# Routing by sequence inside the chunked streams, and expert results normed by sequence beside the shared expert and the last attention

## The chip, the cores and the metric

The kernel runs on one NeuronCore of a Trainium2 chip. The metric is the device time of the whole program in microseconds (us). All times below are in us unless they say otherwise, and times on the profile's clock count from the start of the profiled span.

The engines have short names in the profile: PE multiplies matrices (PEld loads its weights), DVE works on vectors, ACT evaluates activation functions, POOL is the general engine that also issues the indirect transfers, and SP issues most of the other transfers. Each engine takes its instructions in a fixed order and waits for semaphores of the others.

## The reference, cut to what matters

The network has eight layers, each of the form x = layernorm(x + f(x)), in fp32, on 8 sequences of 256 tokens with 128 channels (2048 tokens in all). The sixth layer's f is a chunked attention block, the seventh is a mixture of experts, and then come an attention with 16 heads and a linear layer with ternary weights. The seventh and what surrounds it are what the change touches:

```python
def _L2_ffn_ref(x, router_w, rg, ru, rd, sg, su, sd):
    ...                                   # E, K = 8, 2; capacity = 320 for T = 2048 tokens
    xn = xf * jax.lax.rsqrt(jnp.mean(xf * xf, axis=-1, keepdims=True) + eps)
    logits = xn @ router_w.T
    probs = jax.nn.softmax(logits, axis=-1)
    topk_p, topk_i = jax.lax.top_k(probs, K)
    rw = topk_p / jnp.sum(topk_p, axis=-1, keepdims=True)
    ...
    order = jnp.argsort(~sel, axis=1, stable=True)
    dispatch = order[:, :capacity]        # the first 320 tokens that chose the expert
    ...
    xg = xf[dispatch]
    gate = jax.nn.silu(jnp.einsum('ech,ehi->eci', xg, rg))
    up = jnp.einsum('ech,ehi->eci', xg, ru)
    eout = jnp.einsum('eci,eih->ech', gate * up, rd)
    ...
    routed = jnp.zeros_like(xf).at[dispatch.reshape(-1)].add(contrib.reshape(-1, h))
    shared = jax.nn.silu(x @ sg) * (x @ su) @ sd
    return shared + SCALE * routed.reshape(b, s, h)
...
x = _layernorm(x + _L2_ffn_ref(...), axis=-1)
x = _layernorm(x + _L3_attn_ref(...), axis=-1)
x = _layernorm(x + _L3_ffn_ref(...), axis=-1)
```

A token's place in its expert's list is the number of earlier tokens that chose the same expert. Each token is used by two of eight routed experts (128 to 512 to 128 channels), as long as the place is within the capacity of 320, and by the shared expert (128 to 1024 to 128).

## The kernel before

Activations lie by channel: 128 partitions of channels, 2048 columns of tokens. A tile is 128 tokens, so there are 16 tiles and two per sequence. Six stages run one after the other: `rglru`, `local_mamba`, `moe1`, `chunked`, `moe2`, `typed`. The builder writes a program; a scheduler then sets the order of the instructions on each engine by cost estimates of its own, within the data dependences. `issue_after(later, earlier)` adds an order constraint and `wait_for` a real wait. `psum(tag)` hands out the eight banks of the accumulation memory, split by tags that each stage sets in `BANKS`.

**chunked.** `one_sequence(b)` is one sequence's generator: attention, feed-forward, attention, feed-forward, each followed by a norm. The planner `on_pe` keeps three of them in flight: each `yield` names the PE time of the next piece and how long its result lies behind, and the planner runs the piece that is ready first. The norm by token (`normed`) gives `z`, tokens by channels. `put_rows` writes `z` to a DRAM tensor `rows2` in token order on SP's queue; the sum of squares goes into `ssq` (ACT), and `logits` multiplies the normed activations with the router on PE ("lg") and copies the result into `lg2` (DVE, line 817).

**moe2.** It begins when the last logits are there. On DVE, for all 16 tiles at once, `first_best` takes the best and the second expert, `places` counts places with matmuls "cum" and "tot" and a scan, `slots` turns them into row numbers of the experts' lists, and `dispatch` inverts the map: it compares each place with 128 numbers (line 1115, eight operations of 512 columns) and lets 32 matmuls "which" sum up the token that belongs in each of the 2560 slots. `rows_of` then reads the rows of the tokens from `rows2` by 20 indirect gathers of 128 rows on POOL (line 1147), twelve at first and four after each group, and `group` transposes four of them to channels. Quarters 0 and 1 of the shared expert are issued before the experts. A quarter is `shared(i)`: 512 tokens in 8 chunks, each with the matmuls "pg" and "pu", a silu on ACT and a multiply on DVE (lines 1534 and 1535), and the matmul "acc". The eight experts follow, with their outputs written to `ybuf2` on SP's queue. Then 32 gathers (two per tile) fetch each token's two results. Quarters 2 and 3 of the shared expert run, and `combine` scales and adds the two results of four tiles (lines 1581 and 1582), transposes them (line 1584) and adds them to a quarter's sum; `issue_after` holds these operations behind chunk 4 of the fourth quarter, or a quarter's last. Four layernorms of 512 columns close the stage.

**typed.** Each sequence has six units of scores. In step i of the loop the transposes of unit i-3, the scores of unit i, the softmax of unit i-1 and the outputs of unit i-3 are issued. Between them run side generators, one `next` at two places in the step: `before(b)` (`typed_inputs`: projections "proj", the rotation on DVE with its addition on POOL, the masked keys "km" on POOL, line 1667, and the values) and `after(b, o)` (output projection, layernorm, linear layer, layernorm, output). When the last unit of sequence b is done, `after(b, o)` is appended and `before(b + 2)` behind it. Softmax multiplies its exponentials by 1/sum on POOL (line 1715).

**moe1**, which already routes in parts (`route1`): the rows of each tile are scattered on POOL (line 1058) directly into the experts' places in DRAM, and the places are then read with plain transfers ("got<-places") into the groups.

## Time and profile before

| | us |
|---|---|
| median of 3 runs | 1897.03 (1895.95 to 1901.52) |
| the profiled execution | 1904.73, span 1903.0 |
| mean granted PE clock | 0.91 |
| PE / DVE / ACT / POOL busy in the span | 1571.1 / 1073.6 / 1009.9 / 549.8 |
| last logits of chunked | 1405.6 to 1406.6 |
| routing on DVE | 1406.6 to 1425.8 |
| first expert's first matmul, last expert's last | 1469.4, 1537.0 |
| result gathers | 1540.5 to 1580.2 |
| first scores of typed | 1632.5 |
| scores' start, one sequence to the next, in typed | 33.5 |

The busy time of an engine is the sum of its instructions' durations; PE's instructions overlap, so PE being busy does not mean that it runs at its peak. "Idle before" is the time in which an engine stood ahead of an instruction, with what released it. The granted clock says at what share of the full speed PE's clock ran; a matmul at half clock takes about twice as long.

### The profile page before, as it was taken

The page shows a single profiled execution, that of the slowest core. Times are in us where ns is not written, and L with a number is a line of the kernel's source. Part 1 is how long each engine was busy: PE and PEld are TensorE (multiplying, and loading weights), DVE is VectorE, ACT ScalarE, POOL GpSimd, SP SyncE. Part 2 cuts the span into 40 slices and gives each one's busy share as a digit, 9 for nine tenths or more (in the row PEclk, how much of TensorE's full clock was granted, in tenths as well). Part 3 has the DMA queues.
Part 4 walks back from the last instruction along what each step waited for, and adds up shares of the span by engine and source line. Part 5 has one row for each costly group of instructions (what it writes and reads, how often), then busy time and mean ns, then how long its engine had stood idle before and what let it go on. Part 6 is the DMA issues. An engine that isn't in the chain of part 4 may idle for free. (4 is left out here: it accounts for less than half of the span.)

```text
span 1903.0 us, 28168 instructions
## 1 busy us (share of the span) xinstructions
PE 1571.1 (83%) x10805; PEld 944.4 (50%) x10805; DVE 1073.6 (56%) x1830; ACT 1009.9 (53%) x2657; POOL 549.8 (29%) x483
## 2 busy tenths in 40 slices
PE   3678877887888776786679999999969986898987
PEld 2344544444454433443556666776634642455554
DVE  5734567786878677589224444463452223565654
ACT  4557777676877867454234444554422311454544
POOL 1324452515161414203221010000003042445552
PEclk6689999989999988788789999999979997998998
DMA  3000012121111112266300000000011310000000
GB/s 146 1 1 1 1 35 56 35 56 35 56 41 49 50 41 71 93 198 180 103 24 2 7 7 4 4 4 4 4 37 24 108 39 13 1 4 6 4 7 6
DMA packets 56822, 74.11 MB, mean 39 GB/s; under 512 B 5493, under 2 KB 34360, under 8 KB 55664
## 3 DMA queue, kind: packets, MB, share of 16 engines
q1 hardware_dynamic: 52800, 66.60, 12.0%
q0 software_dynamic: 2832, 5.19, 1.1%
q8 instruction: 85, 1.39, 0.3%
q10 hardware_dynamic: 1056, 0.52, 0.1%
q14 instruction: 49, 0.40, 0.1%
HBM read 65.55 MB, written 7.35 MB: 38 GB/s over the span
## 5 line engine op out<-in xcount | busy, mean ns | idle before, releaser
L396 PE MATMUL y<-hs,ident 128*128 128x512 f32 x256 | 148.4, 710 | 38.3 <-DVE hs L791 38.3
L790 DVE TENSOR_TENSOR_SCAN hs<-da,hs 128x1024 f32<-128x1024 f32 x64 | 148.7, 2332 | 3.5 <-ACT da L786 3.0
L477 PE MATMUL pt<-ident,e 128*128 128x128 f32 x768 | 120.9, 285 | 28.3 <-POOL e L653 17.3
L786 ACT ACTIVATE da<-d,na 128x255 f32<-128x255 f32 x256 | 112.1, 502 | 36.8 <-DVE hs L790 19.3
L653 POOL TENSOR_TENSOR e<-e,rc 128x1024 f32<-128x1024 f32 x32 | 72.2, 2255 | 201.4 <-DVE rc L652 201.3
L1335 POOL TENSOR_TENSOR e<-e,rc 128x512 f32<-128x512 f32 x32 | 33.6, 1052 | 331.9 <-DVE rc L1334 225.6
L1712 ACT ACTIVATE e<-sc,nm 128x128 f32<-128x128 f32 (+1 forms) x256 | 104.2, 435 | 47.7 <-DVE nm L1707 47.2
L648 ACT ACTIVATE e<-sc,nm,rn 128x128 f32<-128x128 f32 x256 | 113.5, 464 | 24.1 <-DVE nm L643 23.9
L1715 POOL TENSOR_TENSOR e<-e,rc 128x1024 f32<-128x1024 f32 x48 | 91.9, 1916 | 111.6 <-DVE rc L1714 73.9
L477 PEld LDWEIGHTS pt<-ident,e 128*128 128x128 f32 x768 | 87.6, 143 | 73.4 <-POOL e L653 24.8
L479 ACT COPY ptsb<-pt 128x512 f32<-128x512 f32 x82 | 48.1, 587 | 141.0 <-PE pt L477 72.5
L600 POOL TENSOR_TENSOR t<-t,t 128x512 f32<-128x512 f32 x64 | 89.1, 1393 | 96.7 <-DVE t L587 88.1
L788 DVE TENSOR_TENSOR hs<-u,bc 128x1024 f32<-128x1024 f32 x64 | 86.5, 1360 | 41.3 <-POOL u L775 26.2
L396 PEld LDWEIGHTS y<-hs,ident 128*128 128x128 f32 x256 | 52.4, 220 | 94.9 <-DVE hs L791 51.7
L1310 ACT COPY kp<-kps 128x512 f32<-128x512 f32 x128 | 74.7, 586 | 41.0 <-PE kps L396 40.8
L479 DVE COPY ptsb<-pt 128x512 f32<-128x512 f32 x110 | 73.7, 683 | 36.6 <-PE pt L477 30.9
L1707 DVE TENSOR_REDUCE nm<-sc 128x4 f32<-128x1024 f32 (+1 forms) x48 | 58.6, 1221 | 51.3 <-PE sc L396 51.2
L396 PE MATMUL qk<-w_local,h 128*128 128x512 f32 x128 | 72.6, 655 | 17.8 <-DVE t L587 13.0
L791 DVE TENSOR_TENSOR hs<-hs,bc 128x1024 f32<-128x1024 f32 x64 | 81.9, 1287 | 0.2
L1534 ACT ACTIVATE sh<-pg 128x512 f32<-128x512 f32 x32 | 19.1, 597 | 102.8 <-PE pg L396 69.2
L1346 DVE COPY vs<-vps 128x512 f32<-128x512 f32 x64 | 42.3, 671 | 52.5 <-PE out L396 31.1
L396 PE MATMUL sc<-km,q 64*128 64x512 f32 x192 | 62.8, 722 | 8.8 <-POOL km L1667 8.7
(425 smaller groups left out, 3797.4 us busy)
## 6 DMA issues: line engine op xcount, KB each, us to landing
bc<-xs SPq DMA_DIRECT2D x128, 256.0 KB
w_attn<-in_w_dram SPq DMA_DIRECT2D x4, 1024.0 KB
w_local<-in_w_dram SPq DMA_DIRECT2D x2, 1557.0 KB
w_moe<-in_e1gate_dram SPq DMA_DIRECT2D x8, 256.0 KB
w_moe<-in_e1up_dram SPq DMA_DIRECT2D x8, 256.0 KB
w_moe<-in_e1down_dram SPq DMA_DIRECT2D x8, 256.0 KB
w_moe<-in_e2rg_dram SPq DMA_DIRECT2D x8, 256.0 KB
w_moe<-in_e2ru_dram SPq DMA_DIRECT2D x8, 256.0 KB
```

The source lines that it names most:

```text
L396: return self.nc.tensor.matmul(out, lhsT, rhs, start=start, stop=stop)
L477: self.last = self.nc.tensor.transpose(pt[:, j * P : (j + 1) * P], src[:, j * P : (j + 1) * P], self.ident)
L479: self.nc.any.tensor_copy(sb.rearrange("p a b -> p (a b)"), pt)
L600: nc.gpsimd.tensor_add(t1, t1, t2)
L648: nc.scalar.activation(e[:, j, g, :], scs[:, j, g, :], AF.Exp, bias=nm[:, j, g : g + 1], scale=rq[:, j, g : g + 1], accum_out=sm[:, j, g : ...
L786: nc.scalar.activation(da[:, n, c, 1:S], d[:, c, 1:S], AF.Exp, scale=na[:, i : i + 1])
L788: nc.vector.tensor_tensor(hs, u.unsqueeze(1).to_broadcast(shp), bn, ALU.mult)
L790: nc.vector.tensor_tensor_scan(line(hs), line(da), line(hs), 0.0, ALU.mult, ALU.add)
L791: nc.vector.tensor_tensor(hs, hs, cn, ALU.mult)
L1310: nc.scalar.copy(k[:, 2 * i : 2 * i + 2, :].rearrange("p a b -> p (a b)"), ps)
L1712: nc.scalar.activation(e[:, i, :], sc[:, i, :], AF.Exp, bias=nm[:, i : i + 1], accum_out=sm[:, i : i + 1])
L1715: nc.gpsimd.tensor_tensor(e, e, rc.unsqueeze(2).to_broadcast([P, n, keys]), ALU.mult)
```

## The change

Four things change.

1. *Routing.* `route2(b, z, work, small)` is called at the end of each sequence in chunked. It scales the logits of two tiles, takes best and second expert, computes places from a running sum over the earlier sequences (`sum2`) with three small matmuls "cum", and scatters the two tiles' rows of `z` twice (four indirect transfers on POOL) into `places[1]` in DRAM. The combined `scatter` serves moe1 as well. `put_rows`, `first_best`, `places`, `slots`, `dispatch` and the gathers of rows go away, and so do their tables. `places[1]` is cleared at the start of the program, as `places[0]` was, by a second transfer of 1280 KB.
2. *Reading the rows.* `rows_of(pool, k)` serves both mixtures: five plain transfers, alternating between SP's and ACT's queue, that wait for all the scatters.
3. *The shared expert.* Its weights are loaded in chunked, into the space of the first attention's folded weights, once the last sequence is past them (`weights_shared`). Quarter 0 is ahead of the experts, quarters 1 to 3 behind.
4. *Results and typed.* `results(b, work)` combines, transposes and norms one sequence (256 columns). Sequence 0's results, the inputs of typed for sequence 0 and sequence 1's results are taken a step at a time between the chunks of quarters 2 and 3; results of b+2 are side generators in typed, appended with the first output unit of sequence b. At the last unit of sequence b the first step of `after` is taken, and `before(b + 2)` is appended ahead of its rest. There are three side steps per unit in place of two. The order of the combining operations is no longer held by `issue_after`. The pools of typed are opened at the start of moe2, so that the memsets of `vm` are in moe2. moe2 has its own split of banks.

```diff
+    def route2(self, b, z, work, small):
+        ...
+        nc.scalar.activation(rs, self.ssq[:, ts], AF.Ln, scale=1.0 / P, bias=float(np.finfo(np.float32).eps))
+        nc.scalar.activation(rs, rs, AF.Exp, scale=-0.5)
+        ...
+        nc.vector.tensor_tensor(lg, lg, each(rs), ALU.mult)
+        for k in range(2):
+            o = oh[:, k]
+            nc.vector.tensor_reduce(mx[:, k], lg, AX.X, ALU.max)
+            nc.vector.tensor_tensor(o, lg, each(mx[:, k]), ALU.is_equal)
+            nc.vector.tensor_tensor(o, o, io, ALU.mult)
+            nc.vector.tensor_reduce(ix[:, k], o, AX.X, ALU.min)
+            nc.vector.tensor_tensor(o, io, each(ix[:, k]), ALU.is_equal)
+            if k == 0:
+                nc.vector.scalar_tensor_tensor(lg, o, NEG, lg, ALU.mult, ALU.add)
+        sel = small.tile([P, 2, E], BF, tag="sel", name="sel", bufs=2)
+        nc.vector.tensor_tensor(sel, oh[:, 0], oh[:, 1], ALU.add)
+        cum = self.psum("M", "cum")[:, 0 : 2 * E].rearrange("p (t e) -> p t e", e=E)
+        self.mm(cum, self.m("upto"), sel, True, False)
+        if b:
+            self.mm(cum, self.onesb, self.sum2.unsqueeze(1).to_broadcast(shp), False, False)
+        self.mm(cum[:, 1, :], self.onesb, sel[:, 0, :], False, True)
+        ...
+        placed = nc.vector.tensor_copy(self.put2[:, :, ts], sc)
+        for t in range(2):
+            for k in range(2):
+                self.scatter(1, z[:, t, :], self.put2[:, k, 2 * b + t : 2 * b + t + 1])
...
     def chunked(self):
...
+                if b == B - 1:
+                    self.weights_shared()
...
-                self.put_rows(b, z.rearrange("p t d -> p (t d)"))
...
                 self.logits(b, y, self.w1[:, 866:874], self.lg2[:, 2 * b : 2 * b + 2, :])
+                self.route2(b, z, work, small)
...
     def moe2(self):
...
-            bt, group = self.rows_of(one, self.rows, self.dispatch(one, [place1, place2], E * CAP))
+            bt, group = self.rows_of(one, 1)
...
-            shared(0)
-            shared(1)
+            for _ in shared(0):
+                pass
...
+            def results(b, work):
+                ps = self.psum("M", "back")
+                for j in range(2):
+                    t = 2 * b + j
+                    r1, r2 = got[t]
+                    nc.vector.tensor_scalar(r1, r1, self.gate2[:, 0, t : t + 1], None, ALU.mult)
+                    nc.vector.scalar_tensor_tensor(r1, r2, self.gate2[:, 1, t : t + 1], r1, ALU.mult, ALU.add)
+                    nc.tensor.transpose(ps[:, j * P : (j + 1) * P], r1, self.ident)
+                s = work.tile([P, S], F32, tag="s", name="s")
+                nc.vector.tensor_add(s, ss[b // 2][:, b % 2 * S : (b % 2 + 1) * S], ps[:, 0:S])
+                yield
+                yield from self.layernorm_steps(work, s, y[:, bass.ts(b, S)], steps=True)
...
-            m, d = shared(2)
-            combine(m, d)
-            m, d = shared(3, combine)
-            combine(m, d)
-            combine(m, d)
+            for _ in shared(1):
+                pass
+            first = chain(results(0, self.ty), self.typed_before(0), results(1, self.ty))
+            for i in (2, 3):
+                for _ in shared(i):
+                    next(first, None)
+            for _ in first:
+                pass
             self.exp_ln()
-            for i in range(4):
-                cs = bass.ts(i, 512)
-                self.layernorm(work, backs[i], y[:, cs])
...
     def typed(self):
...
+            for _ in range(2):
                 if side and next(side[0], True):
                     side.popleft()
             if i >= 3:
                 b, u = units[i - 3]
                 if u[:2] == (0, 0):
                     o = self.psum("O", "o")[:, 0:S]
+                    if b + 2 < B:
+                        side.append(self.results(b + 2, work))
                 self.typed_outputs(u, pts, inputs[b][2], o, last)
                 if u[:2] == (1, 6):
-                    side.append(after(b, o))
+                    rest = after(b, o)
+                    next(rest)
                     if b + 2 < B:
                         side.append(before(b + 2))
+                    side.append(rest)
             if side and next(side[0], True):
                 side.popleft()
...
-BANKS = {..., "typed": dict(A=2, B=2, O=1, M=1)}
+BANKS = {..., "moe2": dict(A=2, B=2, M=3, S=1), "typed": dict(A=2, B=2, O=1, M=1)}
```

## The prediction

> **What bounds the kernel now.** I read the busy shares by window first, then TensorE's timeline, the chain that ended last, and the other engines' timelines around each gap. Columns of the first view: window, its length, busy us (instructions) of PE, PEld, DVE, ACT, POOL, then granted clock, DMA share, GB/s.
>
> ```profile
> 980.00:1380.00 400.00, 392.77 (x4406) 266.94 (x4400) 189.09 (x488) 195.29 (x436) 36.07 (x35) 1.00 0.02 5
> ...
> 1407.00:1425.00 18.00, 9.24 (x42) 3.70 (x42) 16.92 (x64) 2.69 (x4) 0.00 (x0) 0.59 0.23 79
> ...
> 1469.00:1537.00 68.00, 66.92 (x337) 47.20 (x335) 17.05 (x35) 20.07 (x49) 6.61 (x7) 1.00 0.31 83
> 1537.00:1559.00 22.00, 21.76 (x47) 8.02 (x46) 4.81 (x7) 4.81 (x9) 14.16 (x15) 1.00 0.18 50
> 1559.00:1580.00 21.00, 5.62 (x11) 2.35 (x11) 3.93 (x11) 0.60 (x1) 15.91 (x17) 0.64 0.20 53
> ...
> 1606.00:1625.00 19.00, 11.41 (x24) 4.38 (x24) 9.65 (x23) 6.20 (x10) 3.83 (x2) 0.82 0.00 1
> 1625.00:1632.50 7.50, 3.63 (x13) 2.13 (x11) 2.69 (x7) 1.23 (x2) 3.36 (x4) 0.81 0.00 0
> ```
>
> See three things. Chunked (to 1405) is PE alone: 7.2 us idle in 400, at full clock. moe2 has holes: while DVE routes all 16 tiles (1407 to 1425) PE works half the time at clock 0.59; in 1559 to 1580 it works 5.6 of 21 us; four layernorms (1606 to 1625) and the first inputs of typed (to 1632.5) run with nothing beside them. The second hole falls on the 32 result gathers, the first and last of which are
>
> ```profile
> 1540.48 0.94 POOL L1147 DMA_INDIRECT got<-ybuf,s1get  x1 [62.87 <-DMA ybuf<-ys]
> 1541.73 0.94 POOL L1147 DMA_INDIRECT got<-ybuf,s2get  x1 [0.30 <-issue]
> ...
> 1579.21 0.94 POOL L1147 DMA_INDIRECT got<-ybuf,s2get  x1 [0.30 <-issue]
> ```
>
> one per 1.25 us. In typed, PE is stopped once a sequence (start, us, what, and in brackets idle and releaser):
>
> ```profile
> 1716.07 1.13 PE L396 MATMUL proj<-x_moe,w 128*128 128x256 f32 x4
> ...
> 1718.04 1.13 PE L396 MATMUL proj<-x_moe,w 128*128 128x256 f32 x4 [0.41 <-DVE t L1659]
> 1720.02 0.49 PE L396 MATMUL v<-w,x_moe 128*128 128x128 f32 x2 [0.85 <-DVE t L1659]
> 1720.89 0.49 PE L396 MATMUL v<-w,x_moe 128*128 128x128 f32 x2 [0.38 <-DVE vm L1675]
> 1722.80 2.08 PE L396 MATMUL sc<-km,q 64*128 64x512 f32 x4 [1.42 <-POOL km L1667]
> ...
> 1732.00 1.13 PE L396 MATMUL sc<-km,q 64*128 64x512 f32 x4
> ```
>
> The projections come just before they are needed: idle 0.41+0.85+0.38+1.42 = 3.1 us, and then scores at 2.08 for four instead of 1.13.
>
> **The change, step by step.** The instruction order of each engine is that of the built programs.
>
> *Start.* A second 1280 KB clearing goes on SP's queue ahead of the load of the scales, which delays a rotation table on POOL; at the 83 GB/s or more that this queue moves in the experts it is up to 15 us, but the table is first used at 48.5 and was done at 25. 0 to 1 us lost; I take 1. It is 15 if that cover were gone.
>
> *Routing in chunked.* Removed: one 128 KB row write per sequence on SP, which nothing waited for. Added per sequence: about 27 small DVE operations, three tiny ACT ones (0.2 each, tables already loaded: the stage's normalisation uses Ln and Exp too), three PE matmuls "cum", four scatters on POOL. The rows are moe1's routing:
>
> ```profile
> 916.10 0.22 DVE L1029 TENSOR_TENSOR sel<-route_tables,route 128x64 bf16<-128x64 f32 x1
> 916.71 0.23 DVE L1048 TENSOR_TENSOR oh<-cum,sel 128x64 f32<-128x64 f32 x1 [0.30 <-PE cum L396]
> ...
> 917.68 0.17 DVE L1055 CAST put<-route 128x2 int32<-128x2 f32 x1
> 918.60 1.43 POOL L1058 DMA_INDIRECT places<-x_chunked,put  x1 [7.31 <-ACT lg L1080]
> 920.34 0.97 POOL L1058 DMA_INDIRECT places<-x_chunked,put  x1 [0.30 <-issue]
> ```
>
> Scatters: 4 x 1.27 = 5.1 us, hidden: POOL is busy 36 of 400, and its next multiply comes at least 10 us later. DVE: 27 x 0.18 = 5 us, on an engine half idle. The price is PE's: "cum" waits for the selection, 14 chained DVE operations behind the logits at 0.22 to 0.25 = 3.1 to 3.5 us, with 0 to 4.3 us of other DVE work (copies of 0.65, softmax operations of 0.68) between them. PE reaches "cum" 1.7 to 5.6 us after the logits (7 to 77 attention matmuls stand between). So it waits about 2 us per sequence: early ones 5.3 against 2.7; the second and fourth 8 against 5.6; the sixth 3.8 against 1.7. All of PE's queue waits behind it. Seven sequences x (2 + 0.35 for the matmuls) = 16, less some 2 us of other waits (idle 7.2 before) that end meanwhile: D = 14 later at the end of chunked. Bounds: 3 (matmuls alone) and 35.
>
> The Trainium skill ("TensorE: Matmul & The Clock Gate", "What's actually happening") says that the clock halves only after an idle window of about 3.4 us; by that a 2 us wait costs 2 us. The rows above show half speed after idles of at most 1.42 us that sum to 3.1 within 5 us, so the measurement limits the rule: by that row each wait could cost 1.5 more, D = 25. I keep 14, since one 2 us wait in full work is nearer to no loss, and 25 goes into the range.
>
> *moe2 up to the experts.* Let T = 1406.6 + D, the last logits. Only the last two tiles' routing is left: "cum" at T+4; places at T+5.4; scatters T+6.3 to T+11.5. The two reads of the rows on ACT wait for these (T+12.8) and hold the silus queued behind them; the rows land 3.6 us after the issue (922.6 to 926.2 in moe1). The 20 gathers, 32 index matmuls and 8 large compares go; the shared weights, loaded during the last sequence, no longer cost the 2.4 us to the first chunk. One quarter of the shared expert, 8 chunks x 2.83 = 22.6 from T+4.5, and some 5 for the ACT wait and the half clock after it: done at T+32. Experts, unchanged, 67.7: they end at E = 1506+D against 1537, 31-D earlier. But before had two quarters of the shared expert done by then; now only one.
>
> *moe2 after the experts.* First gather at E+3.5 (as before), 40 us for all. Beside them is one quarter, but in DVE's order all 32 combining operations stand between the gate multiplies of that quarter: the fourth multiply waits for tile 3, the eighth for tile 13, the next quarter's first for tile 15. PE waits for the multiplies, so the quarter takes the gathers' time: E+46. Were that order not so, it would be E+23; this is 23 us of price. Then 15 chunks x 2.83 = 42.5; two results and the first inputs between them, 5.5 of PE; clock recovery 2. Table loads: Ln/Exp and silu alternate, 8 loads. The row:
>
> ```profile
> 1410.55 1.28 ACT L1534 ACT_TABLE_LOAD   x1
> 1411.85 0.60 ACT L1534 ACTIVATE sh<-pg 128x512 f32<-128x512 f32 x1
> ```
>
> The skill ("ScalarE: Activation LUTs", "What ACT_TABLE_LOAD costs") adds a drain, 2.66 in all. By the row two loads, a small pair and a silu make 3.5 us against a chunk's 2.83: four times 0.7, about 3. By the page 6.2, less a spare bank's 1: 4 x 2.4 = 10. The next activation stands 0.02 us after the load, so I take 3. First scores at E+99 = 1605+D, against 1632.5: gain 27-D, or 13. The four layernorms (19) and the first inputs (7.6) are thereby off the path; the hold-up takes most of it back.
>
> *typed.* Inputs of b+2 are queued ahead of the rest of the epilogue: some three units earlier, so the stop goes: 3.1 idle + about 1.7 slow matmuls = 4.8, for six sequences 29. Added per sequence: two transposes and two layernorm matmuls, 1.35 of PE (0.53 for a layernorm matmul, 0.15 for a transpose), x6 = 8. DVE 2.4 and ACT 1.2 are hidden (19 and 17 busy of 33). Net 21. Bounds: 5, if the single small PSUM bank or POOL (its "km", 1.9 each, now beside a unit's multiply with 0.8 slack) gives half the stops back; 27 if the added work fits gaps.
>
> **Sum.** -1 +13 +21 = 33 earlier. The profiled execution is 1904.7 (span 1903.0): 1872. The median of the runs is 7.7 below it: 1864.
>
> **Rivals.**
> 1. *Wait at "cum" decides.* Place: seven times in chunked, where any PE wait is end time. Gains elsewhere are 47 - 1; from D = 46, or 6.6 us per wait, it is slower. For: DVE order, and the slow-clock row. Against: nothing between logits and selection waits for work behind "cum", so DVE needs 4 to 8 us, not 10 to 12. Time about 1906.
> 2. *No hold-up.* The gathers outrun the multiplies, or PE's banks cover more: up to 23 earlier, 1842. Against: 1.25 us per gather is steady in both its blocks.
> 3. *typed moves its stop* to POOL or the one small bank: gain 5 instead of 21, 1880. For: POOL's slack of 0.8. Against: POOL is half idle.
> 4. *The change moves work without gain:* D about 25 by the slow-clock row and half of typed: near 1886.
>
> **How the numbers follow.** Chances: forecast 0.50 (own range 1853 to 1875), rival 2 0.13, rival 3 0.15, rival 4 0.12, rival 1 0.10. From these: faster by over 0.3% (which is about what a measurement of this kernel tells from none) 0.86, within it 0.05, taken from the upper parts of rivals 3 and 4 and the lower of 1, slower 0.09. The range 1836 to 1892 leaves out rival 1 and some of 2.
>
> **What would show it.** Right: "cum" on PE with idle of about 2 us released by DVE's selection in each sequence; experts starting some 31-D earlier; acc matmuls of the second quarter spaced by 5 to 7 us and ending near the last gather; eight table loads of 1.28; in typed no idle before scores released by "km", and periods near 30 instead of 33.5. Wrong: waits at "cum" of over 5 us; scatters that hold a multiply on POOL; "km" or the layernorm bank as releaser in typed.

## The result and the profile after

The changed kernel takes 1890.38 us (median of 10 runs, 1888.29 to 1892.98); the kernel before, run beside it on the same chip, takes 1898.38 (10 runs, 1895.42 to 1914.52). The ratio is 0.9947 with an interval of 0.9923 to 0.9970: faster by about half a per cent, where 33 us, or 1.7%, were forecast. The profiled execution took 1891.69, span 1889.9, against 1904.73 and 1903.0: 13 us earlier. The stages below account for these 13 us; the medians differ by 8, because the profiled execution of the kernel before lay 6 above its median.

Windows of the changed kernel (window, its length, busy us and instructions of PE, PEld, DVE, ACT, POOL, granted clock, DMA share, GB/s):

```profile
980.00:1413.00 433.00, 414.18 (x4565) 277.02 (x4568) 222.00 (x708) 202.31 (x462) 61.41 (x61) 0.99 0.03 8
1413.00:1440.00 27.00, 14.53 (x108) 10.92 (x101) 6.68 (x27) 4.93 (x17) 3.66 (x4) 0.64 0.01 2
1440.00:1470.00 30.00, 26.82 (x63) 11.03 (x62) 11.22 (x40) 7.11 (x12) 7.64 (x6) 0.87 0.17 45
1470.00:1540.00 70.00, 69.56 (x340) 47.96 (x340) 16.91 (x34) 21.20 (x52) 0.32 (x1) 1.00 0.27 76
1540.00:1560.00 20.00, 14.24 (x26) 5.49 (x25) 7.39 (x19) 2.39 (x4) 15.12 (x17) 0.84 0.17 49
1560.00:1580.00 20.00, 10.51 (x16) 3.68 (x15) 5.75 (x17) 1.20 (x2) 14.89 (x16) 0.76 0.18 52
...
1600.00:1620.00 20.00, 20.00 (x54) 8.86 (x53) 7.71 (x16) 9.32 (x13) 5.16 (x4) 1.00 0.00 0
```

The hole of the routing is gone (26.8 of 30 busy instead of 9.2 of 18), and so is that of the layernorms (20.0 of 20 instead of 11.4 of 19). But chunked, which had 7.2 us idle in 400, now has 18.8 in 433 and 12.5 more in its last 27, at a clock of 0.64; and beside the gathers (1540 to 1580) PE still works only 25 of 40 us.

For the comparison I cut each profile at the same five events: the first matmul of moe1's results ("back"), the last logits, the end of the last expert, the first scores of typed and the end of PE's last matmul.

| stage, us | before | after | gain | forecast |
|---|---|---|---|---|
| up to moe1's results | 959.4 | 961.9 | -2.5 | -1 |
| chunked, to the last logits | 446.1 | 476.9 | -30.8 | -14 |
| last logits to the experts' end | 131.4 | 97.4 | +34.0 | } +27 |
| experts' end to the first scores | 95.5 | 99.1 | -3.6 | } |
| typed | 265.9 | 250.4 | +15.5 | +21 |

The first row varies between 959 and 972 over the profiles, with nearly the same code ahead of it, so no meaning is given to its 2.5. Of the 20 us by which the profile falls short of the forecast, chunked has lost 17, typed 5 or 6; moe2 gained 3 more than forecast.

**Where chunked lost them.** PE's waits in chunked, before (980 to 1405; what waited, for what: us in total, times, the longest):

```profile
PE out L396 <- ACT ptsb L479: 4.6, 8, 0.7
```

and after (980 to 1420):

```profile
PE out L394 <- ACT ptsb L477: 16.5, 8, 5.0
PE cum L394 <- DVE sel L1042: 2.6, 6, 0.7
```

The wait at "cum", which the forecast put at about 2 us per sequence, is 0.4 on average. A wait that stood in both kernels took its place: attention matmuls that wait for ACT's copy of the transposed exponentials, "ptsb". Where the longest of them falls, POOL's timeline shows the last two of four scatters, PE's the transposes of the exponentials, ACT's the copy (start, us, what, in brackets idle and releaser):

```profile
1415.33 0.97 POOL L1083 DMA_INDIRECT places<-z,put  x1 [0.30 <-issue]
1416.60 0.97 POOL L1083 DMA_INDIRECT places<-z,put  x1 [0.30 <-issue]
```

```profile
1413.55 0.66 PE L475 MATMUL pt<-ident,e 128*128 128x128 f32 x4
1419.19 1.93 PE L394 MATMUL out<-vs,ptsb 128*32 128x128 f32 x32 [4.98 <-ACT ptsb L477]
```

```profile
1418.55 0.59 ACT L477 COPY ptsb<-pt 128x512 f32<-128x512 f32 x1 [5.65 <-remote]
```

PE's transposes end at 1414.21. ACT has been free since 1412.9 and needs nothing else, yet its copy starts at 1418.55: 4.3 us after the transposes, 0.98 after the end of the last scatter (1417.57). The releaser is not given by name ("remote"). The same holds at five other sequences: the last scatter ends at 1087.28, 1144.12, 1199.68, 1256.55 and 1313.30, and the copy starts at 1088.19, 1145.05, 1200.63, 1257.52 and 1314.26, that is 0.91 to 0.97 later each time. After the wait PE works at half clock (1.93 for 32 matmuls that took 1.08 at 1412.32).

The trace says what was late. It also holds the moments at which each engine's semaphore rose (the counter by which an engine tells the others that it has finished something). This copy waits for one semaphore, and only PE raises it: after the transposes that ended at 1411.65 it rose at 1411.66, after those that ended at 1414.21 only at 1418.53. So PE was done and its signal came 4.3 us late. That the row of scatters holds the signal back is at this point a reading of coincidences; the experiments test it.

### The profile page after: what moved, and what is told of

It reads as the page before. It is cut to its first block, busy times and chain, and to the rows that moved or that the text cites. A ratio compares the mean times of both kernels' runs of the same rounds, so it can differ in the third digit from the quotient of the medians.

```text
span 1889.9 us, 28445 instructions
## 1 busy us (share of the span) xinstructions
PE 1575.9 (83%) x10810; PEld 950.7 (50%) x10810; DVE 1089.7 (58%) x2018; ACT 1029.9 (54%) x2703; POOL 564.0 (30%) x493
## 4 chain that ended last, share of the span: by engine, by line
PE 52%; DVE 18%; ACT 11%; POOL 7%; issue 7%; DMA 3%; another core or an unknown queue 1%; SPq 0%; POOLq 0%; DVEq 0%; ACTq 0%
PE sc L394 7%; PE vps L394 6%; PE kps L394 5%; PE pt L475 4%; PE out L394 4%; DVE hs L789 3%; PE o L394 3%; ACT e L647 3%; PE pu L394 3%; PE pg L394 3%; DVE hs L790 2%; DVE hs L787 2%; PE y L394 2%; PE hps L394 2%; PE py L394 2%
## 5 line engine op out<-in xcount | busy, mean ns | idle before, releaser
L475 PE MATMUL pt<-ident,e 128*128 128x128 f32 x768 | 125.0, 289 | 28.3 <-POOL e L652 18.1
L475 PEld LDWEIGHTS pt<-ident,e 128*128 128x128 f32 x768 | 89.7, 146 | 73.6 <-POOL e L652 25.3
L1117 POOL DMA_INDIRECT got<-ybuf,get x48 | 45.6, 951 | 166.1 <-DMA ybuf<-ys 117.0
L1241 DVE BATCH_NORM_STATS2 st<-out 128x6 f32<-128x128 f32 x80 | 20.0, 289 | 91.6 <-PE out L394 84.3
L1304 ACT COPY vs<-vps 128x512 f32<-128x512 f32 x64 | 37.4, 585 | 59.6 <-PE vps L394 51.1
```

The source lines that it names most:

```text
L475: self.last = self.nc.tensor.transpose(pt[:, j * P : (j + 1) * P], src[:, j * P : (j + 1) * P], self.ident)
```

## Experiments

The runs came in five groups. Those of one group shared a chip and the runs of the kernel before on it: chip 15 in the first and fourth group, chips 14, 2 and 6 in the second, third and fifth. The stages are cut as above.

### First group: undo one part, or do one alone

Three versions of the changed kernel and one of the kernel before. *Plain writes* computes the routing in full, and replaces the four scatters by one write of the rows in token order on SP's queue, so that the experts read rows that are not those routed to them; only its time is used.

```diff
-        for t in range(2):
-            for k in range(2):
-                self.scatter(1, z[:, t, :], self.put2[:, k, 2 * b + t : 2 * b + t + 1])
+        i = nc.sync.dma_start(self.places[1][b * S : (b + 1) * S, :].rearrange("(t p) d -> p t d", p=P), z)
+        self.wait_for(i, self.cleared[1])
+        self.scatters[1].append(i)
```

> The changed kernel, with the four scatters per sequence on POOL replaced by one plain 128 KB write of the sequence's normed rows on SP's queue, in token order; so the experts get rows that are not those routed to them, and everything else (routing on DVE, cum on PE, gates, reads, gathers) stays. In the changed kernel the last logits of chunked come 33.3 us later than before, while PE waits only 0.2 to 0.7 us at each cum, and ACT's copies of the transposes (ptsb) go on about 0.95 us after the end of the last of four scatters. Theory S: while POOL's scatters run back to back, a signal of PE reaches ACT late, and the stop costs 2 to 5 us and a spell of half clock per sequence. It expects the last logits 22 to 30 us earlier (near 1409 to 1417), and a time of 1890.4 - 26 = 1864 (1858 to 1870). Theory R: the routing itself (DVE's 27 operations, ACT's three and cum) makes the 33 us. It expects no change beyond 5 us: 1885 to 1891.

*Only scatters* adds to the kernel before four indirect writes of z per sequence into scratch memory, with an index that one DVE operation makes from the logits.

```diff
+                for t in range(2):
+                    nc.vector.scalar_tensor_tensor(put[:, 2 * b + t, :], lg, 0.0, spot[:, 2 * b + t, :], ALU.mult, ALU.add)
+                for t in range(2):
+                    for k in range(2):
+                        nc.gpsimd.indirect_dma_start(
+                            out=scratch[k],
+                            out_offset=bass.IndirectOffsetOnAxis(ap=put[:, 2 * b + t, k : k + 1], axis=0),
+                            in_=z[:, t, :],
...
```

> The kernel before, with only the scatters added: after each sequence's logits, four indirect writes of its rows from POOL to rows of a scratch tensor that nothing reads; one small DVE operation for the indices. No routing in chunked, nothing else changed. Theory S expects the last logits later by about as much as the change did, 15 to 30 us, and a time of 1898.4 + 22 = 1920 (1912 to 1928). Theory R expects 0 to 4 us: 1898 to 1902.

*Results held* orders the two combining operations of each tile behind the multiply of the shared expert (or the softmax's reciprocal) that the builder issued last, which takes them out of the way of the second quarter.

```diff
-                    nc.vector.tensor_mul(h, h, pu)
+                    self.held = nc.vector.tensor_mul(h, h, pu)
...
+                    self.issue_after([i1, i2], self.held)
...
-        nc.vector.reciprocal(rc, sm)
+        self.held = nc.vector.reciprocal(rc, sm)
```

> The changed kernel, with the combining operations of a result on DVE ordered behind the shared expert's multiply (or the softmax's reciprocal in typed) that was emitted just before them, so that none stands between the multiplies of the second quarter. Theory O (that order alone is the hold-up that the prediction priced at 23 us): the second quarter ends at E+23 instead of E+46, the first scores of typed come 23 us earlier (near 1612), time 1890.4 - 23 = 1867 (1862 to 1873). Theory S (late signals of PE while POOL's gathers run, as in the kernel before, where in 1558 to 1586 PE stood without any such order): PE advances until some 14 to 22 gathers are done, then stands until the last has landed; 3 to 4 chunks of 2.83 more are done by then: 1890.4 - 10 = 1880 (1876 to 1885).

*Typed order undone* puts the inputs of b+2 behind the whole of `after` again.

```diff
-                    rest = after(b, o)
-                    next(rest)
+                    side.append(after(b, o))
                     if b + 2 < B:
                         side.append(before(b + 2))
-                    side.append(rest)
```

> The changed kernel, with the side order of typed as before: the epilogue of b first, the inputs of b+2 behind it; three side steps per unit and the results of b+2 stay. The period of typed is 30.7 in the changed kernel and was 33.3 before. If the order is what took the stop at km away, the stop is back: 3 us idle and some slow matmuls in each of six periods, 4 to 5 us each, time 1890.4 + 27 = 1917 (1908 to 1920). If the third side step is what did it, the period stays near 30.7 and the time within 5 us of 1890.

| | chunked | to experts' end | to first scores | typed | median | ratio to before |
|---|---|---|---|---|---|---|
| plain writes | 455.1 | 98.2 | 97.6 | 249.1 | 1872.73 | 0.9822 (0.9768 to 0.9876) |
| only scatters | 450.8 | 135.8 | 94.0 | 263.9 | 1916.48 | 1.0052 (1.0033 to 1.0070) |
| results held | 471.4 | 97.0 | 94.9 | 260.0 | 1895.42 | 0.9931 (0.9900 to 0.9963) |
| order undone | 471.4 | 96.9 | 98.2 | 277.6 | 1913.70 | 1.0033 (1.0013 to 1.0052) |

Three readings. *Plain writes* returns 16 us (to 455.1 from the 471.4 of the two versions beside it that leave chunked alone) and sets the "ptsb" waits (980 to 1420) back to 4.5 us, longest 0.7: the selection chain, the "cum" matmuls and the rest of the routing cost chunked 9 us, the scatters the other 16. But *only scatters* costs 4.7 and not 16, and its "ptsb" waits are 4.6, the longest 0.7, as in the kernel before. It has four scatters per sequence, but not one row of four: POOL's timeline shows two pairs, with a gap where the changed kernel has 0.30.

```profile
1081.14 1.00 POOL L1478 DMA_INDIRECT scratch<-z,put  x1 [0.30 <-issue]
1082.88 0.97 POOL L1478 DMA_INDIRECT scratch<-z,put  x1 [0.74 <-issue]
```

They also meet other work of PE. So this version does not tell whether the gap or the place keeps the waits short. *Order undone* gives the inputs' place its price: 27 us. That is the price in the changed kernel, where the stop at "km" without it is longer (13.5 us in six waits) than in the kernel before (8.7 in seven).

*Results held* was to end the second quarter 20 us earlier. It gained 4. PE's, DVE's and POOL's timelines of this version:

```profile
1571.36 0.63 PE L1532 MATMUL back<-ident,got 128*128 128x128 f32 x2
1571.79 1.91 PE L394 MATMUL pu<-x_chunked,w_shared 128*128 128x512 f32 x2
1582.46 1.22 PE L394 MATMUL ln_mean<-s,mean 128*128 128x256 f32 x2 [8.76 <-DVE s L1534]
```

```profile
1581.98 0.42 DVE L1534 TENSOR_TENSOR s<-s,back 128x256 f32<-128x256 f32 x1 [11.63 <-remote]
```

```profile
1577.24 0.94 POOL L1117 DMA_INDIRECT got<-ybuf,get  x1 [0.30 <-issue]
```

DVE has nothing to do for 11.6 us and its addition needs "back", which PE finished at 1571.99; it starts at 1581.98, 3.8 after the end of the last gather's issue on POOL (1578.18). The combining order is no longer in the way, and yet PE and DVE stand until the gathers are over: as in chunked, PE's signals come late. They do not all wait for the end of the row. ACT's silu, which needs the "pg" that ended at 1562.02, starts 13 us after it, with two gathers still to come:

```profile
1574.98 0.60 ACT L1485 ACTIVATE sh<-pg 128x512 f32<-128x512 f32 x1 [14.13 <-PE pu L394]
```

The kernel before shows the same in the profile from which the forecast was made. There DVE's sum of a quarter needs the "acc" that ended at 1562.68, starts 5.9 us later, and nine gathers are still to come:

```profile
1560.98 1.70 PE L396 MATMUL acc<-sh,w_shared 128*128 128x512 f32 x2 [2.22 <-DVE sh L1535]
1568.56 0.69 DVE L1540 TENSOR_TENSOR s<-acc,x_chunked 128x512 f32<-128x512 f32 x1 [6.33 <-remote]
```

### Second group: loosen the row, on another chip

*Spaced* puts about 1.2 us of memsets between the four scatters, *half* leaves out the second choices' scatters, *later* orders the conversion of the places, and with it the scatters, behind the second maximum of the next attention block. *Gathers paused* is *results held* with some 2.9 us of memsets after each eight gathers. In this order:

```diff
+                if (t, k) != (1, 1):
+                    last = i
+                    for _ in range(4):
+                        m = nc.gpsimd.memset(self.pause, 0.0)      # [128, 192]
+                        self.issue_after([m], last)
+                        last = m
```

```diff
-            for k in range(2):
-                self.scatter(1, z[:, t, :], self.put2[:, k, 2 * b + t : 2 * b + t + 1])
+            self.scatter(1, z[:, t, :], self.put2[:, 0, 2 * b + t : 2 * b + t + 1])
```

```diff
+        def scatters(after=None):
+            placed = nc.vector.tensor_copy(self.put2[:, :, ts], place)
+            if after is not None:
+                self.issue_after([placed], after)
...
```

```diff
+                if t % 4 == 3 and t < NT - 1:
+                    for _ in range(5):
+                        m = nc.gpsimd.memset(pause, 0.0)           # [128, 512]
+                        self.issue_after([m], last)
+                        last = m
```

> The changed kernel, with four short memsets (192 columns each, about 1 us in all) put between each two of a sequence's four scatters on POOL, so that they do not run back to back; a run of scatters takes 8 us instead of 5. From the first matmul of moe1's results to the last logits, chunked took 446 before, 477 in the changed kernel (471 in two others with the same code there), 455 without scatters. Theory H (late signals hold until a row of scatters without a gap has ended, and come through in a gap): the copies behind the transposes are released within 2 us, chunked 455 to 466. Theory L (held as long as any scatter of the four is still to come): the stops grow by 3 us per sequence: 485 to 500.

> The changed kernel, with only the scatters to the best expert (two per sequence instead of four); so the second choices' rows are missing from the experts' places. If the stop is set by the length of the row of scatters, it shrinks by 2.5 us per sequence, and chunked takes 460 to 466 (455 without any, 471 to 477 with four). If one scatter is enough for the whole stop, 470 or more.

> The changed kernel, with the same four scatters per sequence, but issued later: the conversion of the places to integers is ordered on DVE behind the second maximum of the next attention block that is emitted (for some sequences, behind the last norm of the next sequence), so that the scatters meet other work of PE: mostly the long row of value matmuls. The added kernel with scatters alone had them there and lost 4.7 us in all. If the loss comes from where the scatters meet PE's short exchanges with ACT (transposes, copies, outputs), chunked takes 457 to 466 and the time is 1890 - 14 = 1876 (1870 to 1882). If every scatter costs the same wherever it runs, chunked stays at 471 to 477 and the time at 1886 to 1892.

> The kernel with the results held (above), and a pause on POOL of about 2.5 us (five memsets of 512 columns) after each eight gathers of the results. In the kernel with the results held, from the end of the experts to the first scores of typed took 94.9 (99.1 in the changed one); PE kept its pace until 14 gathers were issued and then stood until the last had landed. If a backlog of the gathers holds the signals and a pause clears it, PE keeps its pace: 78 to 86. If not, 95 to 105.

| | chunked | to experts' end | to first scores | typed | time |
|---|---|---|---|---|---|
| spaced | 456.5 | 97.9 | 95.8 | 249.3 | 1867.46 |
| half | 455.9 | 97.1 | 94.1 | 248.9 | 1864.03 |
| later | 456.4 | 97.4 | 94.1 | 249.1 | 1865.98, ratio 0.9898 (0.9881 to 0.9914) |
| gathers paused | 456.6 | 97.2 | 73.6 | 256.9 | 1857.61 |

(Where no ratio is given the time is that of one execution; the kernel before took 1883.49 on this chip.) This group was to tell its versions apart and could not: *gathers paused* does not touch the scatters, and its chunked is as short as that of the other three. On this chip the loss in chunked is simply not there; what is left, about 10 over the 446.1 of before, is the routing. The 73.6 cannot be credited to the pauses either: none of PE's signals is late here, in *later* (94.1) as little as in *gathers paused*, so the pauses had nothing to clear (the count is at the end of the fifth group), and the 20.5 us between the two belong to the combining order. The loss depends on the chip.

### Third group: does it come back?

The changed kernel and the kernel before unchanged, *results held*, and *by chunk*, which issues one tile's combining behind each chunk of quarters 2 and 3, so that typed has no combining held behind its softmax.

```diff
                     held = nc.vector.tensor_mul(h, h, pu)
+                    if i > 1:
+                        combine(8 * (i - 2) + c, held)
```

> The changed kernel as it is, beside others of one call. Of the two calls so far, the one on chip 15 showed late signals in every kernel with indirect transfers (copies behind transposes 2 to 5 us late, chunked 471 to 477), and the one on chip 14 in none (456 to 457 with four, two or moved scatters, and the kernel before at 1883.5 instead of 1895 to 1919). So late signals seem to belong to a chip or its state, and not to where the scatters are. If this call shows no late signals: chunked 456 to 458, from the experts' end to the first scores 94 (the DVE order alone), typed 249, time 0.990 to 0.992 of before. If it shows them: 471 to 477, 97 to 99, and 0.993 to 0.996.

> The kernel before as it is, for its trace on the chip of this call. With no late signals the two last quarters of the shared expert after the experts take 16 chunks of 2.83 = 45 and the first scores come 45 + 19 (layernorms) + 8 (inputs) + 2 = 74 to 80 us after the experts' end, instead of 95.5; time about 1883. With late signals, 95 or more as in the profile shown.

> The kernel with the results held, again. With no late signals theory O alone acts: from the experts' end to the first scores 74 (as with pauses on POOL on chip 14, 73.6), typed 257 since the combining operations then lie in typed, time 0.985 to 0.988 of before. With late signals, 95 and 0.993 to 0.996 as on chip 15.

> The changed kernel, with the two combining operations of tile i ordered on DVE behind the multiply of the i-th chunk of the last two quarters, so that each comes after its gathers have landed (tile i at E+7.4+2.5i, chunk i at E+23+2.8i or later) and none is left for typed. With no late signals: from the experts' end to the first scores 75 to 79 (16 x 0.6 of DVE beside PE), typed 249, so 94 - 77 = 17 to 20 us less than the changed kernel, 0.980 to 0.983 of before. With late signals 95 to 99, no better than the changed kernel.

| | chunked | to experts' end | to first scores | typed | time |
|---|---|---|---|---|---|
| changed | 473.9 | 96.9 | 98.5 | 249.6 | 1891.47, ratio 0.9887 (0.9839 to 0.9935) |
| before | 445.6 | 132.8 | 97.7 | 254.5 | 1904.88, one execution |
| results held | 473.7 | 96.9 | 94.5 | 259.3 | 1895.08, ratio 0.9922 (0.9890 to 0.9954) |
| by chunk | 471.5 | 97.0 | 94.9 | 250.8 | 1882.56, ratio 0.9856 (0.9818 to 0.9893) |

On a third chip chunked is at 472 to 474 again and the combining order is worth 4 us, not 20. The figures repeat those of the first group and of the profile shown to within 3 us, so they do not belong to one chip alone. *By chunk* ends typed's 9 us loss of *results held*; against the changed kernel the stages give it 5 us, and the two intervals overlap.

Typed of the kernel before took 254.5 here and 265.9 in the profile shown; more on this below.

### Fourth group: the same remedies where the loss is

> The changed kernel with pauses between the scatters, again: on chip 14 nothing was late and the run told nothing of a gap. If this call's chip shows late signals: theory H (a gap in the row of scatters lets signals through) expects chunked 456 to 466, theory L (held until the last of the four has ended) 485 to 500; the changed kernel takes 471 to 477 there. With no late signals again 456 to 458.

> The changed kernel with the scatters issued later, again, for a chip with late signals: if where they meet PE's work decides, chunked 457 to 466; if every scatter costs the same, 471 to 477. With no late signals 456 to 458.

> The kernel combined by chunk, with the pause of about 2.5 us on POOL after each eight gathers. On a chip with late signals: if a pause clears them, from the experts' end to the first scores of typed 75 to 80 instead of 94.9, and 15 to 18 us less than 1882.6; if not, 93 to 98 and the same time. With no late signals 75 to 78.

> The kernel combined by chunk, with pauses in the gathers and the scatters issued later. It adds up what the two before it show: chunked as with the scatters later, the rest as with the pauses. On a chip with late signals 0.970 to 0.980 of the kernel before if both help; 0.984 to 0.988 if neither. With no late signals 0.980 to 0.983.

The edits are *spaced*, *later*, *by chunk* with the paused gathers, and that with *later* as well, on the chip of the first group.

| | chunked | to experts' end | to first scores | typed | time |
|---|---|---|---|---|---|
| spaced | 460.5 | 97.9 | 99.2 | 249.7 | 1876.73, one execution |
| later | 464.2 | 96.8 | 101.0 | 249.2 | 1884.69, one execution |
| by chunk, paused | 475.2 | 96.8 | 74.5 | 250.0 | 1867.09, ratio 0.9811 (0.9760 to 0.9861) |
| all three | 467.4 | 96.9 | 74.5 | 250.9 | 1858.87, ratio 0.9768 (0.9720 to 0.9816) |

Now the remedies tell apart, because *by chunk, paused* leaves the scatters as they are and stays at 475.2. Gaps between the same four scatters of the same bytes give back 11 to 15 us of chunked (one execution). PE's waits in *spaced* (975 to 1400):

```profile
PE out L394 <- ACT ptsb L477: 3.4, 6, 0.6
PE vps L394 <- ACT vs L1314: 3.4, 5, 0.9
```

and ACT's and POOL's timelines there, at the sequence where the copy had waited until 1088.19:

```profile
1087.45 0.59 ACT L477 COPY ptsb<-pt 128x512 f32<-128x512 f32 x1 [2.62 <-PE pt L475]
```

```profile
1086.15 1.00 POOL L1092 DMA_INDIRECT places<-z,put  x1 [0.50 <-issue]
1087.13 1.24 POOL L1066 MEMSET pause<- 128x192 f32 x4
1088.84 0.97 POOL L1092 DMA_INDIRECT places<-z,put  x1 [0.47 <-issue]
```

The transposes started at 1086.81, so the copy follows 0.64 later, with two scatters still to come; in the changed kernel it followed 2.38 after them (1085.81 to 1088.19). And the releaser has its name, "PE pt". The second wait is new, and is most of what keeps *spaced* 4 us above its 456.5 on the other chip: single scatters still delay PE's signals, by less than 1 us. *Later* gives back some of the loss (7 to 11 us): three of its rows are broken by a multiply of POOL, and three unbroken ones still make PE's signals 1.4 to 4.5 us late. The pauses between gathers bring the time from experts to first scores from 94.9 (*by chunk* in the third group, *results held* on this chip) to 74.5, which is the 20 that *results held* alone had not brought here. PE in *by chunk, paused* beside the gathers:

```profile
1539.00:1560.00 21.00, 21.00 (x45) 7.59 (x43) 6.19 (x10) 4.18 (x7) 16.65 (x20) 1.00 0.17 44
1560.00:1580.00 20.00, 18.85 (x51) 8.82 (x50) 10.05 (x25) 9.83 (x13) 16.18 (x23) 1.00 0.14 37
```

PE is busy in 39.9 of 41 us. Bandwidth is not what had stopped it: the experts of the changed kernel move 76 GB/s with PE busy 69.6 of 70, more than the 49 and 52 beside its gathers.

### Fifth group: both remedies together, and the kernel before with pauses

> The version that the runs point to: the changed kernel, combined by chunk, with the gathers paused after each eight and the scatters spaced by four short memsets. On a chip with late signals: chunked 460 (with the scatters spaced), from the experts' end to the first scores 74.5 (paused, by chunk), typed 250: span near 965 + 460.5 + 97 + 74.5 + 254 = 1851, 0.972 to 0.976 of the kernel before. With no late signals: chunked 456.5, the same elsewhere, 0.979 to 0.983.

> The kernel before, with the pause of about 2.5 us on POOL after each eight of its 32 result gathers, and nothing else. If the stop of PE in 1558 to 1586 of the profile shown has the cause that the paused gathers showed in the changed kernel, from the experts' end to the first scores shrinks from 95.5 to 78 (74 to 82) on a chip with late signals, time 15 to 19 us less, 0.989 to 0.993 of before. If that stop had another cause, it stays at 93 to 100 and the time within 4 us. With no late signals no change.

| | chunked | to experts' end | to first scores | typed | time |
|---|---|---|---|---|---|
| by chunk, spaced, paused | 456.9 | 97.8 | 72.3 | 248.7 | 1844.07, ratio 0.9796 (0.9780 to 0.9811) |
| before, paused | 446.1 | 130.8 | 75.8 | 265.8 | 1887.29, ratio 1.0017 (1.0004 to 1.0030) |

The first is 2.0% under the kernel before on that chip; the changed kernel itself did not run there. Its chunked:

```profile
980.00:1395.00 415.00, 405.55 (x4516) 273.69 (x4514) 217.28 (x681) 201.15 (x460) 78.80 (x131) 1.00 0.03 9
```

The kernel before gains nothing in time from the same pauses on this chip, although its 75.8 is 20 us under its 95.5 and 97.7 elsewhere. It took 1883.68 without pauses here, 15 to 26 less than beside the result and on the chips of the first, third and fourth group (1898 to 1910). This chip, like that of the second group, does not show the loss, and the 456.9 here cannot be credited to the gaps; the fourth group carries that.

**What the semaphores say of all groups.** PE's semaphore rises 0.01 to 0.09 us after the end of its instruction. Counted here are the rises of PE that came over 0.1 us late, in chunked (from 30 us after its start to the last logits) and from the experts' end to the first scores. Some records are missing beside indirect transfers, so each late rise is put down to the last PE instruction whose own rise is missing: the lateness is a lower bound.

| | chunked, us | late rises in it | longest | sum | late rises after the experts, longest |
|---|---|---|---|---|---|
| kernel before (profile shown, third group) | 446.1, 445.6 | 0, 0 | | | 7 and 7, 2.8 and 8.7 |
| only scatters | 450.8 | 11 | 1.5 | 6.2 | 7, 12.9 |
| plain writes | 455.1 | 0 | | | 4, 7.5 |
| spaced (fourth group) | 460.5 | 11 | 0.7 | 4.1 | 3, 8.6 |
| later (fourth group) | 464.2 | 7 | 4.5 | 8.3 | 4, 8.0 |
| all three (fourth group) | 467.4 | 7 | 4.5 | 8.2 | 0 |
| results held, order undone (first group) | 471.4, 471.4 | 7, 7 | 4.2 | 13.5 | 8 and 3, 9.7 and 3.2 |
| by chunk, results held (third group) | 471.5, 473.7 | 7, 7 | 4.2 | 13.5 | 7 and 10, 7.3 and 9.7 |
| changed (profile shown, third group) | 476.9, 473.9 | 7, 7 | 4.3 | 14.2, 13.4 | 2 and 3, 9.5 and 8.3 |
| by chunk, paused (fourth group) | 475.2 | 7 | 4.4 | 14.4 | 2, 0.2 |
| second and fifth group, all six | 446.1 to 456.9 | 0 | | | 0 |

The changed kernel has seven rows of four scatters before the last logits, and each has one late rise. Without scatters none is late, with gaps the longest is 0.7, and on two chips none is late in any version, from the start of the program to its end. The sums go with the time that chunked loses over the 455.1 of *plain writes*, except in *only scatters*, where PE seldom waits for what is late. No rise of ACT, DVE or POOL is late in any profile. Why chunked took 471.4 in some profiles and 476.9 in another with the same code and the same seven rows is open.

This also answers for the kernel before: its hole at 1559 to 1580 has late signals in both profiles in which it stands, and in *before, paused*, on a chip without them, PE is busy 42.7 of the 43 us from 1537 on. So the delay had a part in the hole (without the pauses this kernel was not profiled on such a chip); the change took over its cause, the unbroken row of 32 gathers.

## Why the prediction was wrong

The sign was right, the size was not: 1864 forecast, 1890 measured, inside the range and at its slow end.

**The step that failed** is "Routing in chunked", in two of its sentences. "Scatters: 4 x 1.27 = 5.1 us, hidden" was right for POOL: no multiply waited for them. But I had asked only what is queued behind them on POOL. In the profile shown and on the chips of the first, third and fourth group PE's signals reach ACT late while the row runs, PE then waits for ACT, and 16 to 22 us went there (471.4 and 476.9 against 455.1 without the scatters; the late signals themselves sum to 13.5 and 14.2, and slow matmuls after the waits come on top). "The price is PE's: cum waits" named the wrong wait: 2.6 us over six sequences instead of 14. The 9 to 11 us that chunked takes more without that loss (plain writes 455.1, the second group 455.9 to 456.6) are less than the forecast 14; of them the "cum" waits (2.2 to 2.6) and their matmuls (7 x 0.35 by the forecast) explain about half, the rest was not taken apart. So D was 30.8 for the forecast 14, near the bound of 35, for a cause that the bound was not made of. Rival 4, "D about 25 and half of typed", came nearest in time (1886), by the wrong mechanism: it took waits at "cum" with slow clock. Rival 1's 6.6 us per "cum" did not occur (its limit adds up to 47, not 46: 27 + 21 - 1).

**moe2 up to the experts** was right. The last "cum" waited 3.0, the two reads on ACT were issued 10.6 after the logits, and the experts ended 97.4 after the logits began, against 100.4. The silus queued behind the reads lost little: one started 0.7 after its matmul instead of 0.04.

**moe2 after the experts** was right as a number, and only half of the reason held. Forecast: gathers make the second quarter last to E+46, first scores at E+99; measured: its last "acc" starts at E+46.5, and the first scores at E+99.1. DVE's timeline shows the combining ahead of the multiply, as forecast, and then something else:

```profile
1576.04 0.35 DVE L1530 SCALAR_TENSOR_TENSOR got<-got,gate 128x128 f32<-128x128 f32 x1 [1.02 <-DMA got<-ybuf,get]
1582.01 0.69 DVE L1486 TENSOR_TENSOR sh<-sh,pu 128x512 f32<-128x512 f32 x1 [5.62 <-remote]
```

The multiply needs "pu", which PE ended at 1574.38, and a silu that ran at 1571.45; DVE is free from 1576.39 and starts at 1582.01. Two causes lay over each other: freeing the order without the pauses gave 4 us, with the pauses 24 to 25 (99.1 to 74.5). "23 us of price" for the order alone was therefore too much on such a chip; on the chip of the second group, where no signal is late, the order is worth 20.5. That the sum came out at E+99 with only one of the two causes in it was luck.

**Table loads** were right:

```profile
1591.92 1.28 ACT L453 ACT_TABLE_LOAD   x1
1593.32 0.39 ACT L453 ACTIVATE ln_rs<-ln_var 128x256 f32<-128x256 f32 x1
1593.72 1.28 ACT L1485 ACT_TABLE_LOAD   x1
1595.02 0.60 ACT L1485 ACTIVATE sh<-pg 128x512 f32<-128x512 f32 x1
```

Eight of them at 1.28, the silu 0.02 after its load; in 1600 to 1620 PE shows no idle at all. The measured row decided correctly against the 2.66 of the Trainium skill ("ScalarE: Activation LUTs", "What ACT_TABLE_LOAD costs").

**typed.** The mechanism was right: "km" is gone from PE's waits, and undoing the order costs 27 us, though with a longer stop than the one that the 29 of the forecast was worked out from. One term was mis-sized: the work added per sequence, 1.35 of PE in the forecast. One period at full clock, first of the kernel before (third group), then of the changed kernel:

```profile
1710.00:1741.00 31.00, 27.95 (x220) 17.39 (x218) 19.17 (x36) 16.93 (x76) 16.95 (x11) 1.00 0.02 5
```

```profile
1709.10:1739.80 30.70, 30.65 (x225) 18.65 (x224) 19.47 (x36) 18.77 (x77) 16.50 (x11) 1.00 0.02 5
```

PE's busy time rises by 2.7. The scores' matmuls in such a period (count, busy, mean ns, idle before), in the same order:

```profile
L396 PE MATMUL sc<-km,q 64*128 64x512 f32 x26 | 7.5, 645 | 2.8 <-POOL km L1667 2.8
```

```profile
L394 PE MATMUL sc<-km,q 64*128 64x512 f32 x24 | 9.0, 641 | 0.0
```

The 26 of the first row include two of the next sequence; its own 24 are six groups of 1.13, that is 6.8. So the scores' matmuls are no more and no longer, but cover 2.2 us more, and PE's timeline of the changed kernel says why:

```profile
1716.66 1.12 PE L394 MATMUL sc<-km,q 64*128 64x512 f32 x2
1717.71 0.70 PE L394 MATMUL ln_mean<-s,mean 128*128 128x256 f32 x2
1718.34 0.69 PE L394 MATMUL sc<-km,q 64*128 64x512 f32 x1
...
1718.87 0.59 PE L394 MATMUL sc<-km,q 64*128 64x512 f32 x1
1722.74 1.13 PE L394 MATMUL sc<-km,q 64*128 64x512 f32 x4
```

Four such matmuls of 64 rows take 1.13 together, at 0.64 each, so they overlap. Where the scheduler put a layernorm matmul between them, two take 1.12 and the other two stand apart; this happens to two of the six groups in a period. The 1.35 of the forecast counted the inserted matmuls by their own length and left out what they break; since neighbours overlap, the 2.7 cannot be split exactly. PE is now busy 30.65 of 30.70: nothing is left to gain there by order.

The gain of typed also depends on what the kernel before does at its stop. It stands idle at the same places in the profile shown and in that of the third group, but in the third group the clock stayed at 1.00 and the period was 30.8, where in the profile shown this was 0.91 and 33.5. Against that execution the change gains 5 us in typed (254.5 to 249.6), not 15.5.

## What to carry to other kernels

A row of indirect transfers that nothing on its own engine waits for is not thereby free: look at what every other engine waits for while it runs, and where a wait with an unnamed releaser falls into the row or ends just after it, break the row with a pause and measure. Such a wait stood in the profile before the change. When two causes end at the same moment, removing one shows almost nothing; remove both before judging either. And count an inserted matmul by what it separates, not only by its own duration.

## What was not expected of the hardware

- While POOL issues indirect transfers back to back (1.25 us each), ACT and DVE can see PE's results late: in six sequences the waiting copy starts 0.91 to 0.98 us after the end of the last of four scatters; beside the 32 gathers results came up to 13 us late, some while the gathers ran and some 2.6 and 3.8 us after the last. Transfers' own releases get through meanwhile (the combining on DVE at 1576.04 above), and so do the signals of ACT and DVE. Scatters with gaps of 1.7 us still show it, by under 1 us; with 2.9 us of memsets after each eight gathers 0.2 or less was counted. Which part of the chip holds the signal, and how the delay grows with the length of a row, is open.
- It depends on the chip: chunked of kernels with four unspaced scatters at the place of the changed kernel took 471 to 477 in the profile shown and on the chips of the first, third and fourth group, 456.6 on that of the second, and there and on the chip of the fifth no signal of PE was late. What differs between the chips is open.
- The clock fell in some executions and not in another after the same idles (at most 1.42, 3.1 in all within 5 us). The page of the Trainium skill that the prediction set against this row ("TensorE: Matmul & The Clock Gate", "What's actually happening") names an idle window of about 3.4 us as what halves the clock; of two profiles of the kernel before, the one shown fell to half speed without such an idle and that of the third group did not, and what decides is open.
